# Output projection and last layer of an attention block from rounded fp32 pairs to norm-scaled fp16 pairs

## The chip, the cores and the metric

One NeuronCore of one Trainium2 chip runs the whole kernel. The metric is the device time of one execution in microseconds; of several executions the median is taken. The kernel before needs 1552.88 us (three executions, 1550.75 to 1553.57).

The engines are named as in the profile: PE is TensorE's matmuls and PEld its weight loads, DVE is VectorE, ACT is ScalarE, POOL is GpSimd, SP is SyncE, which issues most DMAs. SBUF is the on-chip memory and PSUM the memory into which PE writes.

## What is computed

One block of multi-head latent attention (2048 positions, width 512, 16 heads), followed by a residual and layer norm, a linear layer, and a residual and layer norm again. All inputs and outputs are fp32.

```python
cq  = rms_norm(x @ w_qa.T, q_a_ln_w);   q = (cq @ w_qb.T)            # 16 heads x (128 + 64 rotary)
ckv = x @ w_kva.T;                      ckv_l = rms_norm(ckv[..., :128], kv_a_ln_w)
k_nope, v = split(ckv_l @ w_kvb.T)      # 16 heads x (128 + 128)
attn = softmax(causal(q_full @ k_full.T * 192 ** -0.5))
a = concat_heads(attn @ v) @ w_o.T
x = layernorm(x + a)
w = ffn_weight * scale_weight[:, None]
x = layernorm(x + x @ w.T + bias)
```

The kernel uses a rearranged form. The values of all heads are one latent matrix (128 wide), so each head's attention is taken over the latent rows, and value weight and output weight of a head are multiplied together once (`wvo`, 128 x 512 a head).

## The kernel before

**Pairs.** Every large product is made of two numbers for each operand: a high part `h`, which is the operand rounded to the product's type, and a low part `l`, the rest. Three products high x high, high x low and low x high are added in PSUM. Projections, scores and values use fp16 pairs, scaled so that both parts fit fp16's range: `split16` (L66) lets ACT write `h = scale * src` and DVE write `l = scale * src - h`. The output stage and the last layer use pairs of F32R, a rounded fp32 type: `split` (L71) does the same with a plain subtraction (L75), or with a scale (L77, L78).

**Order of the work.** The 2048 rows are handled in four blocks of 512 (`b`), the 16 heads in eight pairs (`p`). `units` (L896) runs attention for one block: for each pair and each of four tiles of 128 rows (`qt`), scores (L618), maximum (L655), exp (L670), the split of the normalized probabilities (L691 on ACT, L694 on DVE), a DMA that transposes them on SP's queue (L698), and, three such steps later, the products with the latent values (L747). The result of each pair goes to DRAM (`ot_d`). From block 1 on PE and SP execute in the written order; the order on ACT, DVE and POOL is made by the planner of the framework, except that from the second step of block 3 ACT and DVE are in written order too. DMAs handed to `put_off` wait in a list and are issued on SP's queue by `put_in`, after the next transpose.

**The output stage** starts inside the last pair of block 3. `value_output` (L281) multiplies value and output weight of a pair and splits the result into `wvo`; `latent_load` (L999) brings a pair's attention result back, into one of two buffers `o`, and `latent_split` (L1003) splits it into `oh` and `ol`, two buffers of each, or, for pairs 4 to 7 of the last block, into eight tiles of their own (`ohl`). `accumulate` (L1042) adds a pair to one of four PSUM tiles `acc` of 128 rows x 512: six products of 128x512 (L1046), three for each head.

In each block all pairs are added to the four tiles, pair by pair. The last block does so for pairs 0 and 1 only (`CUT = 2`); for the rest it goes tile by tile, so that the tiles end one after the other.

**The last layer.** When a tile is full, `residual` (L1133) adds the input rows, `first_norm` normalizes them (`layer_norm`, L1124: statistics on DVE, the inverse root on POOL, scaling on DVE), and `ffn` (L1144) is appended to a list `late`. It has two steps that `advance` (L1165) runs at written places between accumulation products: first four transposes by PE (L1147) and the split `xt`, then twelve products (L1157), residual (L1159), layer norm and the DMA out (L1161). The weights `fw` are scaled, loaded and split by `load_fw` (L1118) in four pieces after pairs 4 to 7 of the first block.

## Time and profile before

| view | value |
|---|---|
| median of three executions | 1552.88 us |
| profiled execution | 1551.89 us |
| its span, first to last instruction | 1550.1 us |
| granted TensorE clock, mean | 0.987 |
| busy share: PE, PEld, DVE, ACT, POOL | 96%, 65%, 75%, 60%, 22% |
| PE accumulation L1046: `oh`, `ol`, `ohl` | 144.0 us x448, 88.1 us x224, 24.5 us x96 |
| PE last layer L1157 | 46.7 us x192 |
| PE weight products L286 | 16.1 us x32 |
| ACT exp L670 | 324.0 us x320 |
| SP's DMA queue, share of 16 DMA engines | 69.4% |

Busy times of PE overlap, because matmuls are pipelined and their ends are modelled: a matmul of 128x512 is listed with some 0.4 us and starts 0.2 us after the one before. For PE, times from start to start are what to read. Times of the other engines are those of one instruction. An idle time is put down to the work that ended last before the engine went on.

### The profile page before, as it was taken

The numbers are of one execution on the slowest core, as the hardware profiler recorded it, in microseconds if no ns is written. First come the engines' busy times: TensorE is split into PE (matmuls) and PEld (weight loads), VectorE is DVE, ScalarE is ACT, GpSimd is POOL, SyncE is SP. The second block draws the span as 40 slices with busy tenths as digits, with TensorE's granted clock in tenths as the row PEclk, the third lists the DMA queues.
The fourth block names the chain that finished last, engine by engine and source line by source line (L and its number), as shares of the span: only waits on it lengthen the run. The fifth ranks groups of instructions, "written<-read, shape, count | busy, mean of one in ns | idle before, by whom it ended". The sixth has DMA issues, their size and how long they took to land. (4 is left out here: it accounts for less than half of the span.)

```text
span 1550.1 us, 24523 instructions
## 1 busy us (share of the span) xinstructions
PE 1488.9 (96%) x9100; PEld 1000.6 (65%) x9100; DVE 1164.4 (75%) x2181; ACT 927.3 (60%) x1684; POOL 344.5 (22%) x398
## 2 busy tenths in 40 slices
PE   8889888999999999999999999999999999999997
PEld 6667664666665566666665665665566656788886
DVE  4887788888888888888896777777777775455564
ACT  6677775766675777767766666666666664321120
POOL 4223211441306304050052202201300000032132
PEclk9899999999999999999999999999999999999999
DMA  5556465878897988878986887786788798433230
GB/s 198 147 137 180 129 165 117 154 152 165 167 189 143 169 164 154 159 149 160 197 152 131 154 154 145 145 163 134 145 163 179 145 217 206 140 122 117 95 116 34
DMA packets 614872, 234.56 MB, mean 151 GB/s; under 512 B 569696, under 2 KB 593248, under 8 KB 614112
## 3 DMA queue, kind: packets, MB, share of 16 engines
q1 hardware_dynamic: 613440, 231.26, 69.4%
q8 instruction: 71, 1.16, 0.3%
q10 hardware_dynamic: 1008, 1.18, 0.3%
q0 software_dynamic: 304, 0.56, 0.1%
q14 instruction: 49, 0.40, 0.1%
HBM read 62.33 MB, written 28.05 MB: 58 GB/s over the span
## 5 line engine op out<-in xcount | busy, mean ns | idle before, releaser
L618 PE MATMUL s<-Kn,qn 128*128 128x512 f16 (+5 forms) x1920 | 465.2, 349 | 25.3 <-ACT pr L670 14.3
L670 ACT ACTIVATE pr<-s,bias,er 128x1024 f32<-128x1024 f32 (+3 forms) x320 | 324.0, 1015 | 210.6 <-DVE bias L664 161.8
L694 DVE SCALAR_TENSOR_TENSOR hl<-pr,inv,hl 128x1024 f16<-128x1024 f32 (+7 forms) x320 | 354.0, 1119 | 40.1 <-ACT hl L691 35.9
L747 PEld LDWEIGHTS <-V 128*128 128x128 f16 x3264 | 319.0, 98 | 80.8 <-issue 6.6
L747 PE MATMUL o<-ring,V 128*128 128x256 f16 x3024 | 361.0, 273 | 0.3 <-DVE qn L69 0.3
L691 ACT ACTIVATE hl<-pr,inv 128x1024 f16<-128x1024 f32 (+7 forms) x320 | 294.3, 960 | 80.6 <-ACT pr L670 34.3
L618 PE MATMUL s<-Kp,pe 128*128 128x512 f16 (+5 forms) x1280 | 342.1, 349 | 0.0
L655 DVE TENSOR_REDUCE neg<-s 128x1 f32<-128x1024 f32 (+3 forms) x320 | 317.2, 991 | 17.6 <-PE s L618 14.4
L618 PEld LDWEIGHTS <-qn 128*128 128x128 f16 x1920 | 188.3, 98 | 173.5 <-issue 34.9
L618 PEld LDWEIGHTS <-pe 128*128 128x128 f16 x1280 | 125.4, 98 | 106.4 <-issue 0.5
L576 PE MATMUL ps_qn<-cq,wq 128*128 128x512 f16 (+1 forms) x594 | 141.2, 386 | 5.9 <-DVE inv L680 2.2
L1046 PE MATMUL acc<-wvo,oh 128*128 128x512 f32 x448 | 144.0, 402 | 2.0 <-ACT pr L670 2.0
L565 POOL TENSOR_TENSOR pe<-prod,ph 32x512 f16<-32x512 f32 x88 | 121.7, 1383 | 5.7
L558 POOL TENSOR_TENSOR prod<-prod 128x512 f32<-128x512 f32 x11 | 14.0, 1269 | 465.6 <-DVE prod L502 465.6
L576 PEld LDWEIGHTS <-wq 128*128 128x128 f16 x594 | 60.2, 102 | 70.0 <-issue 13.3
L682 DVE TENSOR_SCALAR inv<-sums 128x1 f32<-128x1 f32 x128 | 27.0, 211 | 101.0 <-ACT pr L670 100.6
L1046 PEld LDWEIGHTS acc<-wvo,oh 128*128 128x128 f32 x448 | 83.1, 188 | 23.5 <-issue 3.8
L1046 PE MATMUL acc<-wvo,ol 128*128 128x512 f32 x224 | 88.1, 393 | 0.0
L564 POOL CAST pe<-prod 32x512 f16<-32x512 f32 x88 | 68.7, 781 | 13.8 <-PE o L747 10.4
L497 PE MATMUL ps_pe<-cq,wpe 128*128 128x512 f16 (+1 forms) x306 | 69.5, 372 | 1.2 <-DVE wpe L69 0.9
L74 ACT ACTIVATE oh<-o 128x1024 fp32r<-128x1024 f32 x28 | 29.7, 1060 | 65.9 <-PE acc L1046 48.6
L752 ACT ACTIVATE ot<-o 128x256 f32<-128x256 f32 x128 | 48.2, 377 | 34.8 <-PE o L747 25.9
(180 smaller groups left out, 1589.6 us busy)
## 6 DMA issues: line engine op xcount, KB each, us to landing
ot_d<-ot SPq DMA_DIRECT2D x128, 128.0 KB, 2.4
o<-ot_d SPq DMA_DIRECT2D x32, 512.0 KB, 3.6
wq<-wq_d SPq DMA_DIRECT2D x30, 384.0 KB, 3.8
wpe<-wpe_d SPq DMA_DIRECT2D x15, 384.0 KB, 3.8
wo<-in_wo_dram SPq DMA_DIRECT2D x4, 1024.0 KB, 5.5
x<-in_x_dram SPq DMA_DIRECT2D x16, 256.0 KB, 3.9
out_dram<-xb SPq DMA_DIRECT2D x16, 256.0 KB, 2.0
xr<-in_xT_dram SPq DMA_DIRECT2D x12, 256.0 KB, 3.5
```

What stands on the lines that cost most here:

```text
L497: nc.tensor.matmul(ps, w[:, i, lt, x * P : (x + 1) * P], cq[:, k, lt, cols], start=n == 0, stop=n == 3 * LT - 1)
L564: nc.gpsimd.tensor_copy(pe[32 * x : 32 * x + 32, j, :], rp[q, x, :])
L565: nc.gpsimd.tensor_tensor(pe[64 + 32 * x : 96 + 32 * x, j, :], rp[q, x, :], ph[q, 0, x, :], ALU.subtract)
L576: nc.tensor.matmul(ps, w[:, i, lt, j * P : (j + 1) * P], cq[:, k, lt, cols], start=n == 0, stop=n == 3 * LT - 1)
L618: nc.tensor.matmul(ps[:, :w], lhs, K[:, i, c0 : c0 + w], start=n == 0, stop=n == 4)
L655: nc.vector.tensor_reduce(neg[:, ti : ti + 1], v, axis=AX.XY, op=ALU.max, negate=True)
L670: nc.scalar.activation(pr[:, c0 : c0 + n * w].rearrange("p (a c) -> p a c", a=n), v, AF.Exp, bias=bias, scale=r, accum_out=sums[:, ti : ti ...
L691: nc.scalar.activation(hl[:, 0, c], pr[:, c], AF.Copy, scale=inv)
L694: nc.vector.scalar_tensor_tensor(hl[:, 1, c], pr[:, c], inv, hl[:, 0, c], ALU.mult, ALU.subtract)
L747: nc.tensor.matmul(ps[:, :256], vt[:, i, k % 4, :], v[:, :, l, k, :], start=n == 0, stop=n == 3 * kts - 1)
L752: nc.scalar.activation(ot, ps[:, :256], AF.Copy)
L1046: nc.tensor.matmul(acc, l[:, t, c], state["wvo"][p][:, i, j, :], start=p == 0 and j == 0 and n == 0, stop=p == NPAIR - 1 and j == 1 and n ...
```

## The change

Names and line numbers are those of the kernel before.

*Scales.* The new pairs are fp16, so each operand gets a scale from a norm. The attention result is scaled by `kvo` = key/value norm weight / its norm x 2^-12, `wvo` by `wscale` = 32768 / (norm of all value weights x norm of all output weights), the last layer's weights by `fscale` = 32768 / their norm, and its input by 1024. The products of these scales are taken back in `residual` (`back`) and after the last layer's products (`fback`).

```diff
+    kvo, wscale, back, fscale, fback = ...   # const tiles [P, 1] F32, in place of kvln_o
         root(kvn, tot)
+        rk = small.tile([P, 1], F32, tag="rf", name="rk")
+        nc.vector.reciprocal(rk, kvn)
+        nc.vector.tensor_scalar(kvo, kvln, rk, O_DOWN, ALU.mult, ALU.mult)
```

*Norms of the output weights.* A new generator reads both weights once more, in ten pieces of 128x1024 (512 KB). One step runs after the second head of each step `qt` of block 1, from pair 2 on. Its pool `nw` has two buffers and lives in block 1.

```diff
+    def output_norms(pool):
+        pieces = [a["wv"][:, 8 * i : 8 * i + 8] for i in range(2)] + [a["wo"][:, 2 * i : 2 * i + 2] for i in range(8)]
+        sums = small.tile([P, 10], F32, tag="osum", name="osum", bufs=1)
+        held = []
+        for n in range(len(pieces) + 1):
+            if n < len(pieces):
+                w = pool.tile([P, 1024], F32, tag="nw", name=f"nw{n}")
+                put_off(w.rearrange("p (a c) -> p a c", a=8 if n < 2 else 2), pieces[n])
+                held.append(w)
+            if n:
+                w = held.pop(0)
+                nc.scalar.activation(w, w, AF.Square, accum_out=sums[:, n - 1 : n])
+            yield
+        yield
+        ps = psum["m"].tile([P, 512], F32, tag="m", name="ps_on")
+        nc.tensor.matmul(ps[:, :10], ones, sums, start=True, stop=True)
...
+            root(f[:, i : i + 1], tot[:, i : i + 1])
...
+        nc.vector.reciprocal(r, f)
+        nc.vector.tensor_scalar(wscale, r[:, 0:1], r[:, 1:2], W_O, ALU.mult, ALU.mult)
+        nc.vector.tensor_scalar(back, f[:, 0:1], f[:, 1:2], kvn, ALU.mult, ALU.mult)
...
+                        if b == 1 and p >= 2 and j == 1:
+                            next(norms, None)
```

*Splits.* All F32R tiles of this stage become F16 (`wvo`, `oh`, `ol`, `ohl`, `fw`, `xt`). In the last block pairs 2 to 7 have tiles of their own, not 4 to 7.

```diff
-            split(ps, wvo[:, 0, j, :], wvo[:, 1, j, :], kvln_o)
+            split16(ps, wvo[:, 0, j, :], wvo[:, 1, j, :], wscale)
-        if b == NB - 1 and p >= 4:
+        if b == NB - 1 and p >= 2:
-        split(state.pop(("o", b, p)), oh, ol)
+        split16(state.pop(("o", b, p)), oh, ol, kvo)
```

*Last layer's weights.* `load_fw` becomes a generator of four steps, run after pairs 4 to 7 of the first block: the four loads into a tile of their own; four multiplications and four Squares; the norm; the four splits.

```diff
+        for kt in range(KT):
+            nc.vector.tensor_tensor(fraw[:, kt], fraw[:, kt], fsc, ALU.mult)
+            sq = pc.tile([P, HID], F32, tag="xb", name=f"fsq{kt}", bufs=2)
+            nc.scalar.activation(sq, fraw[:, kt], AF.Square, accum_out=sums[:, kt : kt + 1])
+        yield
+        ps = ps_f.tile([P, HID], F32, tag="ff", name="ps_fn")
+        nc.tensor.matmul(ps[:, :KT], ones, sums, start=True, stop=True)
...
+            split16(fraw[:, kt], fw[:, 0, kt, :], fw[:, 1, kt, :], fscale)
```

*Residual, norm and last layer in `n` parts.* `parts(n)` cuts the 512 columns into `n` slices. `layer_norm` takes statistics and writes its result part by part. The last layer's products go through all high x high and high x low terms first and through low x high after them.

```diff
-        nc.vector.tensor_tensor(x, acc, x, ALU.add)
+        for i, c in enumerate(parts(n)):
+            nc.vector.scalar_tensor_tensor(x[:, c], acc if n == 1 else acc[i], back, x[:, c], ALU.mult, ALU.add)
...
+        for c in range(0, KT, KT // cuts):
+            k4 = slice(c, c + KT // cuts)
+            for kt in range(c, c + KT // cuts):
+                nc.tensor.transpose(pt[:, kt, :], x1[:, kt * P : (kt + 1) * P], ident)
+            split16(pt[:, k4], xt[:, 0, k4], xt[:, 1, k4], X_UP)
...
+        terms = [(l, i, kt) for ls in (((0, 0), (0, 1)), ((1, 0),)) for kt in range(KT) for l, i in ls]
+        for c in parts(cuts):
+            for n, (l, i, kt) in enumerate(terms):
+                nc.tensor.matmul(
+                    ps[:, c], xt[:, l, kt, :], fw[:, i, kt, c], start=n == 0, stop=n == len(terms) - 1
+                )
+            nc.vector.scalar_tensor_tensor(xb[:, c], ps[:, c], fback, xb[:, c], ALU.mult, ALU.add)
+        layer_norm(xb, xb, cuts)
+        for n, c in enumerate(parts(cuts)):
+            (nc.scalar if n else nc.sync).dma_start(out[0, t * P : (t + 1) * P, c], xb[:, c])
```

*The last 128 rows.* In the last block pairs 0 and 1 are added to three tiles. The fourth is filled at the end, in two halves of columns, each in a PSUM tile of its own and with all eight pairs; the two steps of the row tile before run between them.

```diff
-                for t in range(4):
+                for t in range(3 if last else 4):
                     accumulate(accs[t], p, t, *cuts[b, p])
...
-            for t in range(4):
+            for t in range(3):
                 for i, p in enumerate(range(CUT, NPAIR)):
                     accumulate(accs[t], p, t, *cuts[b, p])
...
+            ends = [accs[3], ps_a.tile([P, HID], F32, tag="acc", name="acc3_4")]
+            for i, c in enumerate(parts(2)):
+                for p in range(NPAIR):
+                    accumulate(ends[i], p, 3, *cuts[b, p], c)
+                    if (i, p) in ((0, 6), (1, 2)):
+                        advance()
+            halves = [ends[i][:, c] for i, c in enumerate(parts(2))]
+            late.append(ffn(4 * b + 3, first_norm(b, 3, residual(b, 3, halves, 2), 2), 2))
```

## The prediction

> **What bounds the kernel now.** I read the page's slices first, then the stretches of the output stage, then the chain of waits in order of time, then the timeline of TensorE (PE).
>
> ```profile
> span 1550.1 us, 24523 instructions
> ...
> PE   8889888999999999999999999999999999999997
> ...
> DVE  4887788888888888888896777777777775455564
> ACT  6677775766675777767766666666666664321120
> ```
>
> PE is the bound nearly everywhere. After slice 33 (about 1290 us) ACT and DVE fall to half or less and PE stays at 9: the output stage. Its stretches, columns PE, PEld, DVE, ACT, POOL busy, granted clock, DMA share, GB/s:
>
> ```profile
> 1367.07:1424.04 56.97, 56.97 (x258) 46.65 (x257) 30.44 (x44) 10.89 (x12) 12.45 (x20) 1.00 0.35 111
> 1424.04:1480.80 56.76, 56.76 (x256) 46.48 (x255) 30.23 (x44) 10.89 (x12) 12.44 (x20) 1.00 0.34 111
> 1480.80:1535.74 54.94, 54.42 (x252) 44.43 (x251) 28.77 (x50) 9.27 (x12) 14.46 (x23) 1.00 0.22 75
> 1535.74:1550.10 14.36, 6.62 (x28) 4.40 (x26) 6.84 (x13) 0.60 (x1) 3.61 (x7) 0.95 0.10 37
> ```
>
> The first runs from one block's first transposes to the next block's, so it holds one block: 192 accumulation products (L1046), 48 of the last layer (L1157), 16 transposes (L1147). PE has no idle time in it and the clock is full. In all 54.94 us of the third there is one short wait, and only the last 14.4 us are a chain over several engines. So the price of this stage is the pitch of its products, start to start. The chain and the timeline give both pitches:
>
> ```profile
> 1343.65 23.41 PE acc L1046 x102
> 1367.07 0.44 PE tp L1147 x4
> ```
>
> ```profile
> 1281.52 0.81 PE L618 MATMUL s<-Kn,qn 128*128 128x512 f16 x3
> 1282.17 0.59 PE L618 MATMUL s<-Kp,pe 128*128 128x512 f16 x2
> 1282.60 0.81 PE L618 MATMUL s<-Kn,qn 128*128 128x512 f16 x3
> ```
>
> Rounded fp32: 23.41/102 = 0.2295; over the whole block (56.97 - 4 x 0.44)/240 = 0.2300 us. The fp16 score products, also 128x512 and also with a new weight load for each, start five in 1282.60 - 1281.52 = 1.08: 0.216 us.
>
> **The change, part by part.** The sum is made against the profiled execution: 1551.9 us, of which 1550.1 are the span, 1.0 under the median of 1552.9.
>
> *Pitch.* Between 1293.43 (from where the chain stays with PE and its feeders) and the end of the accumulation at 1535.5 lie 762 of the 768 accumulation products (six are earlier) and 180 of 192 of the last layer (12 come in the tail). 942 x (0.2300 - 0.2160) = **-13.2**. The transposes (L1147) and weight products (L286) stay fp32 and cost what they did. ACT does one 128x1024 copy per split as before (L74, 1.06). DVE does a scalar_tensor_tensor in place of a subtraction: 1.27 (L694, 128x1024) against 1.23 in the last blocks; the scaled residual 0.75 (L78) against 0.69. DVE is busy 30 of 57 us there, so these 0.1 us cost nothing; without that cover, 28 late splits and 16 residuals would be about 2 us.
>
> The Trainium skill speaks against this term: "TensorE: Matmul & The Clock Gate", section "Step-by-step: what each phase is for", has a stream of products cost "purely `N cycles`", and its specifications name the same 512 columns for all types; by that both kinds would take N/2.4 plus about 2.5 ns = 0.216 us and this term would be 0. The fp16 rows agree with it and the rounded fp32 rows do not, so I go by the rows.
>
> *Norm scales in block 1.* New: ten loads of 512 KB on SP's queue, ten ACT Squares of 128x1024, one small PE product, two reductions, six further DVE operations of one column, four on POOL. Exps of block 1 start every 3.63 us (24 from 317.6 to 404.8), so a pair of heads is 7.27 us, of which ACT is busy 56.21/85.00 = 66%: 4.8 us, 2.5 spare. A Square is about 1.1 plus 0.19 for its sum (L691 and L670): 1.25 with overlap. One per pair fits into the spare, if its load has landed. It is issued behind a transpose (1.5 us on SP) and the Square follows one head later; at 3.6 us to landing (o<-ot_d, also 512 KB) the Square waits 1.5 + 3.6 - 3.63 = 1.5, and what is queued behind it is the next head's exp, whose PSUM tile PE waits for. Ten times (1.5 + 1.25 - 2.5) = 2.5; with a Square placed after the landing, 0. I take **+1.5**. The loads also crowd the transposes: 5.24 MB at the 284 GB/s moved at share 0.89 (1300 to 1320) are 16.4 us of all queues, on 0.83 x 85 = 71: 87 of 85. The 2 us of backlog stay under the three pairs (22 us) by which values trail scores; without that lag they would cost 2. PE's small product comes two pairs after the last Square, and the scales are first used near 1255; POOL's and DVE's parts hide behind that.
>
> *Last layer's norm.* Four Squares (0.69 + 0.19) and one PE product between the sixth and seventh pair of block 0, where a pair takes 5.5 us and the chain of four multiplications (0.69 each) and the last Square takes 3.6. Fits, with **+0.3** for the product itself; up to 3 if DVE's queue has splits ahead. The fp16 splits follow at about 1357, first use is at 1370. The start gets two DVE operations more: **+0.2**.
>
> *Last block.* In the third stretch PE now reaches pair 2 earlier: twelve products (2.6 us) of the last 128 rows move behind all others, on top of the pitch. Its feeders are also freed: pairs 2 and 3 get their own split tiles and wait for no product. Counted from block 2's end, a load (3.5) and its split (1.06 + 1.23) take 6 us in each of two buffers; pair 5 is split at 17 while PE asks at 15, pair 7 at 23 against 21. In place of the one wait (0.5 by the waits, 0.7 in starts) I expect 1.5: **+0.8**, between -0.7 and +2.
>
> *Tail.* Before, the last twelve last-layer products of the row before ran at 1535.5 to 1538.3, under the DVE and POOL chain. Now both steps of it come before the end of the accumulation: 12 x 0.216 = +2.6 on PE's path. The last accumulation in halves costs 96 x 0.109 (L747, 256 columns) against 48 x 0.216: **+0.1**. After it the residual and statistics work on half of the columns (0.44 + 0.42 against 0.70 + 0.70): -0.5. The normalized halves, turns, splits, products and second residual could overlap by halves, but each of the two PSUM tiles is one bank. What the trace shows of such a bank is this:
>
> ```profile
> 12.57 0.28 DVE L331 COPY kvr<-ps_kv 128x128 f32<-128x128 f32 x1
> ...
> 12.88 0.22 ACT L334 ACTIVATE junk<-ps_kv 128x64 bf16<-128x64 f32 x1 [0.92 <-DVE kvr L331]
> ...
> 13.23 0.29 DVE L336 TENSOR_TENSOR rot<-ps_kv,csk 128x128 f32<-128x128 f32 x1 [0.38 <-ACT junk L334]
> ```
>
> Two engines that only read different columns of one tile take turns. If PE takes turns too, its second pair of turns waits for the first half's ACT and DVE (0.38 + 0.44), and its second half of products for DVE's 0.44. Worked through from the first norm's start, PE's products end at 5.8 us (before: 1538.37 to 1543.67, 5.3); then 0.44 + 0.42 in place of 0.70 + 0.70, and two half norms, 0.76, for one of 0.55: 8.7 against 8.5. With full overlap it would be about 7.0. So the tail is +2.6 - 0.5 + 0.2 = **+2.3**, between +0.6 (overlap) and +5 (if PE, idle for 2.6 us, restarts at the 0.50 clock of the first 12 to 14 us and its 24 products double). The row is two readers, not a writer, but it is the nearest, so I take turns.
>
> On the writer the Trainium skill has a rule, "PSUM — Partial Sum Buffer", section "PSUM bank collisions raise a hardware error": guard by bank and quadrant, not by address, for writers as for readers. By it the tail is +2.3, without it +0.6; no row before shows a PE write beside a read.
>
> Sum: -13.2 + 1.5 + 0.3 + 0.2 + 0.8 + 0.1 + 2.3 = -8.0: 1543.9 on the profiled execution, 1544.9 on the median. I forecast **1544.5**.
>
> **The rivals.**
> 1. *The halves do overlap* (0.15): tail +0.6, so 1542.8. For it: the two halves of the residual have separate banks. Against it: the rows above.
> 2. *The feeders become the bound* (0.12): loads, ACT and DVE fall behind in the blocks. For it: ACT waited 4.00 us for a load at 1302.92, and for products only because it was ahead; in the last block the margins are 1 to 2 us. Against it: ACT is at 19% in a full block. Four more microseconds: 1548.5.
> 3. *Squares block ACT* (0.08), the slower side: in block 1 a load lands after 6.6 us (the 512 KB load of cs there), not 3.6. Each Square then waits 4.5 us with exps behind it; ten times (4.5 + 1.25 - 2.5) = 32, less the three score tiles that PE runs ahead (10.9): +21 in place of 1.5, so 1564. For it: loads go behind transposes on one queue that is 0.83 full. Against it: ACT's order there is planned, not written out. It makes the kernel slower from a wait of 2.4 us per Square on: 10 x (2.4 + 1.25 - 2.5) = 11.5 against the 9.5 that the rest gains.
> 4. *The pitch isn't the type's* (0.05): accumulation stays at 0.230 for a reason of the stage, and the change brings only its costs: 1552.9 + 5.2 = 1558. Against it: L618 and L576 hold 0.216 with the same shape in the same kernel.
>
> **How the numbers follow.** My forecast has 0.60. A measurement of this kernel can't tell less than 0.2% (3.1 us) from no change. Faster: forecast 0.59, rival 1 0.15, half of rival 2 0.06: 0.80. Slower: rivals 3 and 4 but 0.02 that end within the bound, and 0.01 of the forecast: 0.12. The rest, 0.08, is no change. The range reaches from all bounds at their good end (-13.2 - 0.7 + 0.6 + 0.3 + 0.1 = -12.9, and 1 us of spread: 1539) to feeders and tail at their bad end (1551).
>
> **What would show it.** L1046 and L1157 at 0.216 start to start, blocks of some 53.6 us; ACT Squares in block 1 with waits for loads under 2 us and no PE wait behind them; one wait of 1 to 2 us in the last block; a tail of about 14 us from the last accumulation product, with PE and DVE in turns on the last tile. I am wrong if the pitch stays, if ACT waits longer for the loads, or if other blocks of attention change by more than 2 us.

## The result, and the profile after

| | before | changed |
|---|---|---|
| median, 17 executions each, in turns | 1552.88 us | 1556.01 us |
| lowest to highest | 1550.66 to 1554.55 | 1552.96 to 1559.17 |
| profiled execution, span | 1551.89, 1550.1 | 1558.61, 1556.8 |

The ratio is 1.0025, with a 95% interval of 1.0018 to 1.0032: slower by 3.1 us in the medians. Of all executions below one, 1710.69 us of `g2_const_halves` at a granted clock of 0.846, was in a slower state and is left out. Forecast were 1544.5 and a range of 1539 to 1551. The profiled execution of the changed kernel lies 2.6 us above its median, and that of the kernel before 1.0 below, so its parts sum to more than 3.1.

The page of the changed kernel, the slices of its span (40, tenths):

```profile
span 1556.8 us, 24722 instructions
...
PE   8889888998999999999999999999999998999997
...
DVE  5887787887888888888887777777777775465564
ACT  6677675666765776767775665665666665422220
```

PE falls to 8 in slice 10 (350 to 389 us), which was full before; the 8 in slice 34 is the start of the output stage, with waits that the kernel before has too. To see where the program falls behind, I paired each score product (L657 now, L618 before) with its like in the other trace; the written order of PE gives every one the same place in both:

| stretch, by the time before | started later by, in the stretch |
|---|---|
| up to 347 us | +0.35 |
| 347 to 435 us: block 1, where the Squares run | **+10.17** |
| 435 to 1261 us: the rest of attention | +0.57 |
| output stage (what is left of the span) | **-4.39** |

**Block 1.** The stretch of the Squares before and after (columns: PE, PEld, DVE, ACT, POOL busy, granted clock, DMA share, GB/s), and ACT's waits in it:

```profile
319.00:404.00 85.00, 85.00 (x556) 54.13 (x554) 72.66 (x155) 56.21 (x90) 38.28 (x36) 1.00 0.83 157
```

```profile
319.00:404.00 85.00, 76.10 (x487) 47.19 (x485) 65.91 (x137) 59.03 (x98) 33.66 (x33) 1.00 0.99 202
```

```profile
ACT nw L311 <- DMA nw<-in_wo_dram: 11.1, 8, 2.8
...
ACT nw L311 <- DMA nw<-in_wv_dram: 4.7, 2, 3.0
```

PE had no idle time and now has 8.9 us. All ten Squares wait for their loads, 15.8 us together. ACT's timeline shows what stands behind such a wait (the bracket is the idle time before, and what ended it):

```profile
370.77 1.08 ACT L709 ACTIVATE pr<-s,bias,er 128x896 f32<-128x896 f32 x1
...
374.71 1.06 ACT L311 ACTIVATE nw<-nw 128x1024 f32<-128x1024 f32 x1 [2.76 <-DMA nw<-in_wo_dram]
...
375.77 1.02 ACT L730 ACTIVATE hl<-pr,inv 128x896 f16<-128x896 f32 x1
376.70 1.18 ACT L709 ACTIVATE pr<-s,bias,er 128x1024 f32<-128x1024 f32 x1
```

The exp that starts at 376.70 had nothing left to wait for; it stood behind the Square. Behind that exp ACT has the copy `ot` of a finished value product, and this copy is what PE waits for next:

```profile
378.30 1.14 PE L786 MATMUL o<-ring,V 128*128 128x256 f16 x9 [1.57 <-ACT ot L791]
```

**Output stage.** One full block, from its first transposes to the next block's, and the last block around its wait; then the chain of waits:

```profile
1375.64:1429.19 53.55, 53.55 (x259) 25.33 (x257) 29.73 (x45) 11.58 (x12) 15.79 (x25) 1.00 0.38 123
...
1481.00:1485.00 4.00, 4.00 (x12) 1.48 (x11) 2.50 (x3) 1.49 (x2) 3.42 (x4) 0.58 0.68 203
```

```profile
1405.88 23.31 PE acc L1087 x108
1429.19 0.44 PE tp L1220 x4
```

A block takes 53.55 us where it took 56.97, and 23.31/108 = 0.2158 us is the pitch of a product: the gain is there. It is given back behind it. In the last block (ACT, DVE and PE):

```profile
1474.46 1.15 ACT L71 ACTIVATE ohl<-o,kvo 128x1024 f16<-128x1024 f32 x1 [4.99 <-DMA o<-ot_d]
...
1475.51 1.13 ACT L71 ACTIVATE oh<-o,kvo 128x1024 f16<-128x1024 f32 x1
...
1478.41 2.28 DVE L72 SCALAR_TENSOR_TENSOR ol<-o,kvo,oh 128x1024 f16<-128x1024 f32 x1
...
1480.75 0.39 PE L1087 MATMUL acc<-wvo,ol 128*128 128x512 f16 x1 [2.76 <-DVE ol L72]
```

ACT splits pair 2 (`ohl`) ahead of pair 1 (`oh`), which PE needs first; PE waits 2.76 us, and for the next four microseconds the granted clock is 0.58: some eight products start 0.427 us apart instead of 0.216, 1.7 us. The end:

```profile
1535.01 2.75 PE L1229 MATMUL ff<-fw,xt 128*128 128x512 f16 x12
...
1541.08 0.48 DVE L1206 SCALAR_TENSOR_TENSOR x<-acc,back,x 128x256 f32<-128x256 f32 x1
...
1543.81 0.66 PE L1220 MATMUL tp<-ident,x 128*128 128x128 f32 x2 [2.77 <-DVE x L1200]
...
1544.93 0.42 DVE L72 SCALAR_TENSOR_TENSOR xt<-tp,xt 128x256 f16<-128x256 f32 x1 [0.94 <-ACT xt L71]
1545.41 0.69 PE L1220 MATMUL tp<-ident,x 128*128 128x128 f32 x2 [0.93 <-DVE xt L72]
1545.89 2.77 PE L1229 MATMUL ff<-fw,xt 128*128 128x256 f16 x12
...
1549.30 1.74 PE L1229 MATMUL ff<-fw,xt 128*128 128x256 f16 x12 [0.64 <-DVE xb L1232]
...
1553.24 0.73 DVE L1200 TENSOR_SCALAR xb<-xb,mv,lnr 128x256 f32<-128x256 f32 x2 [0.98 <-POOL lnr L332]
```

The twelve products of the row before run at 1535.01, ahead of the end. The halves take turns: the second pair of transposes waits 0.93 us for DVE, which reads other columns of the same tile, and the second twelve products wait 0.64. From the last residual to the last norm it is 12.90 us, before 11.13.

### The profile page after: what moved, and what is told of

Its sections match the earlier page's. It is cut to its first block, busy times and chain, and to the rows that moved or that the text cites. A ratio compares the mean times of both kernels' runs of the same rounds, so it can differ in the third digit from the quotient of the medians.

```text
span 1556.8 us, 24722 instructions
## 1 busy us (share of the span) xinstructions
PE 1481.7 (95%) x9164; PEld 923.4 (59%) x9164; DVE 1169.7 (75%) x2199; ACT 941.9 (61%) x1713; POOL 352.2 (23%) x404
## 5 line engine op out<-in xcount | busy, mean ns | idle before, releaser
L657 PE MATMUL s<-Kn,qn 128*128 128x512 f16 (+5 forms) x1920 | 466.0, 349 | 26.2 <-ACT pr L709 15.7
L657 PE MATMUL s<-Kp,pe 128*128 128x512 f16 (+5 forms) x1280 | 342.6, 350 | 0.0
L657 PEld LDWEIGHTS <-qn 128*128 128x128 f16 x1920 | 188.3, 98 | 175.5 <-issue 36.3
L657 PEld LDWEIGHTS <-pe 128*128 128x128 f16 x1280 | 125.4, 98 | 106.8 <-issue 0.3
L1087 PE MATMUL acc<-wvo,oh 128*128 128x512 f16 (+1 forms) x424 | 125.7, 379 | 2.1 <-ACT pr L709 2.1
L1087 PE MATMUL acc<-wvo,ol 128*128 128x512 f16 (+1 forms) x212 | 80.2, 378 | 2.8 <-DVE ol L72 2.8
L1087 PEld LDWEIGHTS <-oh 128*128 128x128 f16 x424 | 41.7, 99 | 51.4 <-issue 8.3
L603 POOL CAST pe<-prod 32x512 f16<-32x512 f32 x88 | 68.8, 782 | 14.7 <-PE o L786 11.3
L71 ACT ACTIVATE xt<-tp 128x512 f16<-128x512 f32 (+1 forms) x17 | 9.7, 571 | 91.8 <-PE tp L1220 85.5
```

Source lines behind the costliest of these rows:

```text
L603: nc.gpsimd.tensor_copy(pe[32 * x : 32 * x + 32, j, :], rp[q, x, :])
L657: nc.tensor.matmul(ps[:, :w], lhs, K[:, i, c0 : c0 + w], start=n == 0, stop=n == 4)
L1087: nc.tensor.matmul(acc[:, cols], l[:, t, c], state["wvo"][p][:, i, j, cols], start=p == 0 and j == 0 and n == 0, stop=p == NPAIR - 1 and j ...
```

## The experiments

Each run is set beside executions of the kernel before on the same chip (medians 1552.2 to 1553.0). "Block 1", "rest" and "output" are the stretches of the table above; "chain" is the time from the start of the last residual to the end of the last norm. The stretch up to 347 us, in which these kernels differ by less than the spread, varied from -2.2 to +0.6.

| run | median us | ratio, 95% interval | block 1 | rest | output | chain |
|---|---|---|---|---|---|---|
| changed kernel | 1556.01 | 1.0025 [1.0018, 1.0032] | +10.2 | +0.6 | -4.4 | 12.9 |
| n1_const | 1546.91 | 0.9969 [0.996, 0.9979] | 0.0 | +0.6 | -4.2 | 13.2 |
| n3_loads | 1546.59 | 0.9964 [0.995, 0.9977] | +1.0 | -1.2 | -4.1 | 13.1 |
| n4_squares | 1545.43 | 0.996 [0.9947, 0.9973] | +0.1 | +0.2 | -4.0 | 13.0 |
| n2_lag | 1554.61 | 1.0015 [1.0005, 1.0025] | +9.2 | -2.0 | -4.0 | 13.2 |
| n5_lag_pin | 1550.23 | 0.9984 [0.9976, 0.9993] | +5.2 | -0.9 | -5.0 | 13.0 |
| t1_tail | 1549.93 | 0.998 [0.9971, 0.999] | +9.4 | -1.4 | -11.5 | 11.3 |
| t2_pin | 1554.76 | 1.001 [1.0001, 1.0019] | +10.4 | -0.1 | -8.1 | 12.2 |
| c0_plain | 1542.92 | 0.9939 [0.9926, 0.9952] | 0.0 | 0.0 | -7.2 | 13.0 |
| b0_on_later | 1555.26 | 1.0014 [1.0005, 1.0023] | +1.4 | +8.5 | -4.0 | 12.4 |
| b1_both | 1549.10 | 0.9971 [0.9958, 0.9983] | +1.2 | +6.5 | -11.4 | 11.3 |
| b2_const_tail | 1540.74 | 0.992 [0.9908, 0.9933] | 0.0 | +1.1 | -11.5 | 11.3 |
| b3_halves | 1550.60 | 0.9986 [0.9977, 0.9995] | +1.6 | +8.6 | -10.1 | 9.7 |
| f0_order | 1573.25 | 1.0137 [1.0124, 1.015] | +9.2 | +16.2 | -4.8 | 12.4 |
| f3_full | 1566.41 | 1.0093 [1.008, 1.0106] | +9.8 | +17.4 | -10.6 | 13.0 |
| f2_halves | 1565.57 | 1.0081 [1.0068, 1.0094] | +9.3 | +17.6 | -12.0 | 9.7 |
| g2_const_halves | 1540.29 | 0.9925 [0.9912, 0.9938] | 0.0 | +1.1 | -12.5 | 9.7 |
| h1_lag_full | 1544.78 | 0.995 [0.9936, 0.9963] | +5.6 | -0.8 | -11.8 | 11.3 |
| h2_lag_halves | 1543.50 | 0.9949 [0.9936, 0.9961] | +5.4 | -1.2 | -12.7 | 9.7 |

### Block 1: loads, Squares, or the wait between them

Theory: ACT, which works in order, is parked on loads that have not landed. Rivals: the ten loads crowd the DMA queues, or the Squares' own 12.5 us of ACT work is too much. `n1_const` has neither loads, Squares nor their norm (the scales come from two constants); `n3_loads` keeps the loads and leaves the Squares out; `n4_squares` squares a tile of ones ten times and loads nothing:

```diff
+        nc.vector.memset(wscale, W_O / (45.254834 * 22.627417))   # n1_const, in place of the whole generator
...
-                nc.scalar.activation(w, w, AF.Square, accum_out=sums[:, n - 1 : n])   # left out in n3_loads
...
-                put_off(w.rearrange("p (a c) -> p a c", a=8 if n < 2 else 2), pieces[n])   # left out in n4_squares
```

> Leaves out the norms of the two output weights: no loads, no Squares, no product for them in block 1; the two scales come from constants. If block 1's norm work costs what the trace of the changed kernel shows there (scores 10.5 us late by the end of block 1), the time falls by 9 to 11 us from 1556.0 to 1545 to 1547, and scores of block 2 start within 1 us of the kernel before. If that delay came from elsewhere in the change (a different plan of the order because of new tiles and scales), it stays near 1556.

> Leaves out the Squares; the ten loads are kept and read by nobody, the sums are constants. If the loads' crowding of the transposes on SP's queue is the cost, scores stay 5 to 10 us late and the time near 1556. If ACT's waits or work are the cost, the time falls to 1545 to 1548.

> Leaves out the ten loads; ten Squares of the same size run at the same places on a tile of ones, which no transfer fills. If ACT's work is the cost, the time stays near 1556. If only the wait for the landing is, the time falls to 1545 to 1548. In between, each Square costs what exceeds ACT's 2.5 us of spare per pair of heads.

Without both, block 1 loses nothing and the kernel is 1546.91 us, 9.1 less than the changed kernel. The loads alone are nearly free, +1.0. The windows row of that run:

```profile
319.00:404.00 85.00, 84.53 (x552) 53.76 (x550) 71.41 (x151) 55.33 (x89) 38.28 (x36) 1.00 1.09 216
```

The queues are as busy as in the changed kernel, or busier (1.09 against 0.99), and PE still has 84.53 of 85. So the loads by themselves are not the cost.

`n4_squares` doesn't answer its half of the question, though its time (1545.43) is in the range set for it. Its Squares on ACT (the durations are least, median and most in ns, then the starts of the first and the last):

```profile
L312 ACT ACTIVATE nsq<-one x10: 1045/1062/1092, 204.6 to 229.9; 128x1024 f32<-128x1024 f32 x10
```

With no load to wait for, the planner put them into block 0, some 130 us earlier than in the changed kernel. Block 1 of that run has neither loads nor Squares, so its +0.1 says nothing about Squares there. What is left is the wait or the Squares' work in block 1. If it is the wait, Squares that come later must be nearly free. Two runs put each one step later (three buffers `nw`); the second also holds it to its place in the program:

```diff
-            if n:
+            if n > 1:
-                nc.scalar.activation(w, w, AF.Square, accum_out=sums[:, n - 1 : n])
+                tc.keep_in_program_order(nc.scalar.activation(..., accum_out=sums[:, n - 2 : n - 1]))  # n5 only
```

> The Square of a piece is issued one step (7.3 us) later, with three buffers in place of two; the same loads and Squares. If ACT's wait for the landing, with exps behind it, is the cost (15.8 us of ACT waits in ten Squares), the waits fall under 2 us in all and the time falls by 8 us or more, to 1546 to 1548. If ACT's own work on the Squares (12.4 us) or the crowded DMA queues are the cost, waits fall but the time stays within 2 us of 1556.

> As n2_lag, and each Square is also held behind what is written before it on ACT. (In n2_lag the ten Squares stand at the same ten places of ACT's order as in the changed kernel: the planner puts them where it takes the load as landed.) Here nine of ten stand four to eight ACT instructions later, with all loads and Squares kept. If a Square's wait for its load, with exps behind it, is the cost, ACT's 15.8 us of waits fall below 4 us and the time falls by 7 to 10 us from 1556.0, to 1546 to 1549. If loads and Squares together are too much for block 1 without any wait, it stays above 1553.

`n2_lag` still waits 15.9 us and loses 9.2: in ACT's program the ten Squares stand within one place of where they stood. The reading that fits: the planner puts an instruction where its model takes the operands as ready, whatever the program's order, and in the model the loads (4.2 to 5.3 us to landing in the changed kernel's trace) land earlier. The Squares of `n4_squares`, ready at once and 130 us early, fit it too; the model itself no run shows. Held in place, no Square waits, and up to 408 us, with all ten Squares done, the loss is 1.3. The rest, 3.9, comes at 412 us, from a new place (PE's timeline; the stretch after it):

```profile
412.44 0.39 PE L315 MATMUL ps_on<-osum,ones 128*128 128x10 f32 x2 [1.86 <-DVE qn L72]
```

```profile
412.40:417.00 4.60, 4.56 (x23) 2.65 (x24) 2.73 (x10) 2.30 (x5) 2.27 (x4) 0.67 1.02 205
```

The ones product of the norms takes a PSUM tile of `m` whose last reader, DVE's split of `qn`, is 1.86 us late; then the clock is 0.67 for some microseconds.

### The ones product elsewhere

`b0_on_later` is `n5_lag_pin` with one more `yield` ahead of the ones product, so that it comes a step later. `f0_order` holds the Squares in program order without the lag and runs the product in block 3:

```diff
-        yield   # left out in f0_order; b0_on_later has one more
         ps = psum["m"].tile([P, 512], F32, tag="m", name="ps_on")
...
-                        if b == 1 and p >= 2 and j == 1:
+                        if b == 1 and 8 <= 4 * p + qt < 19 and j == 1 or (b, p, qt, j) == (3, 2, 0, 1):   # f0_order
```

> The changed kernel with the Squares one step later and held in program order (as in the run before with both), and the ones product of the norms (L315) one step later still, away from the step whose fill has just taken the PSUM tiles of 'm'. Theory: what block 1 still lost in that run was this product's wait of 1.86 us for a PSUM tile, and the slower clock behind it: the scores then reach 414 us at most 2 us later than before (there 5.2), and the time falls by 2.5 to 4 us, from 1550.2 to about 1546.5. Rival: the rest comes from the ten loads or from the Squares' 12.4 us of work, not from the product's place: scores at +4 to +5 and 1549 to 1551.

> The changed kernel with the Squares held in program order, not put one step later, and the ones product taken out of block 1 into block 3 (third pair). The order of ACT then differs from the kernel without norms in 10 rows, all in block 1, against 42 up to the last block in the run with the product one step later. Theory: the losses at 507 and 850 us came from that order, and are gone: the scores at 1261 us stand at most 2 us behind the kernel before's, and the time is that of the constants (1546.9) plus 0 to 2, 1547 to 1549. Rival: the Squares now stand where their loads (4.4 to 6.0 us to landing) have not landed, or the product in block 3 waits as it did in block 1: 1550 to 1553.

`b0_on_later` met its expectation in block 1 (+1.4), and that answers the question left above. Three runs have all ten loads and all ten Squares in block 1 and no Square that waits: `b0_on_later` loses 1.4 there, `b1_both` 1.2 and `b3_halves` 1.6 (the last two are described below), of which the loads alone were 1.0. Where the Squares wait, 15.8 us together in the changed kernel, 15.9 in `n2_lag`, 11.0 in `f0_order` and 12.7 in `f3_full`, block 1 loses 9.2 to 10.2. So it is the wait.

The time of `b0_on_later` missed by 9 us: the score products fall back 4.7 us by 507 us and 6 us at 834 to 846, in blocks that the edit doesn't touch. ACT and PE at the first place:

```profile
498.52 1.44 ACT L731 ACTIVATE hl<-pr,inv 128x576 f16<-128x576 f32 x2 [1.94 <-DMA ring<-hl]
```

```profile
505.09 1.23 PE L658 MATMUL s<-Kn,qn 128*128 128x512 f16 x3 [2.34 <-ACT pr L710]
```

Before, the next head's exp stood ahead of these splits. Now they come first and ACT is parked until a transpose has left their buffer; DVE's low half waits 2.31 us behind it, the next maxima behind that, and their exps are late. Against `n5_lag_pin`, ACT's order differs between 414 and 545 us and nowhere else, for one `yield` some 90 us before the loss; PE's order is the same there. That cannot be the cause of the second loss, 300 us later. There the first exp of block 3 waits, in `b0_on_later` and then in `n5_lag_pin`:

```profile
843.81 1.20 ACT L710 ACTIVATE pr<-s,bias,er 128x1024 f32<-128x1024 f32 x1 [6.47 <-DMA ring<-hl]
```

```profile
836.34 1.20 ACT L709 ACTIVATE pr<-s,bias,er 128x1024 f32<-128x1024 f32 x1 [1.16 <-DMA ring<-hl]
```

The first waits for the last transpose of block 2, the second for the one before it. `b1_both` has the long wait too (6.39 us). Why the exp waits for another transfer in these runs stays open.

`f0_order` shows both halves at full size. Block 1 loses 9.2 again, with 11.0 us of Squares waiting: held in order but without the lag, they come too early. Its rival, a wait in block 3, came far dearer than the 3 to 6 us set for both: the rest of attention loses 16.2. PE at the ones product, then DVE, then POOL, then PE again:

```profile
968.76 0.60 PE L314 MATMUL ps_on<-osum,ones 128*128 128x10 f32 x2 [5.25 <-DVE prod L540]
```

```profile
969.48 0.15 DVE L317 TENSOR_REDUCE otot<-ps_on 128x1 f32<-128x8 f32 x1
987.51 0.17 DVE L322 RECIPROCAL or<-of 128x2 f32<-128x2 f32 x1 [17.88 <-POOL of L166]
```

```profile
976.65 9.64 POOL L603 TENSOR_TENSOR pe<-prod,ph 32x512 f16<-32x512 f32 x8
986.37 1.10 POOL L166 TENSOR_TENSOR of<-rt_t,half 128x1 f32<-128x1 f32 x2
```

```profile
993.04 1.12 PE L656 MATMUL s<-Kn,qn 128*128 128x384 f16 x3 [11.04 <-ACT pr L708]
```

The ones product itself waits 5.25 us for its PSUM tile. Then DVE is parked for 17.88 us on a root of one column that POOL has queued behind eight operations on `pe` (9.64 us); the maxima, and so the exps, and so PE's score tiles stand behind it, and PE waits 11.04 us. The two waits make the 16.2. But the losses at 507 and 844 us are gone (the score products stay at +8.8 from 435 to 941), though loads and Squares are in block 1 as before, and ACT's order departs from that of `n1_const` in block 1 only. So the norms by themselves don't bring those losses. For the one at 507 us the order that the theory named fits; what brings the one at 844 us, these runs don't show.

### The last 128 rows

`t1_tail` gives the last 128 rows the order of the kernel before (full width, pairs 0 and 1 not put off, the step of the row before behind the end); own tiles for pairs 2 to 7 stay. `t2_pin` is the changed kernel with ACT's split of pair 2 held behind that of pair 1. `c0_plain` has the constants, the old end, and own tiles for pairs 4 to 7 only; `b2_const_tail` the same with 2 to 7.

```diff
-                for t in range(3 if last else 4):
+                for t in range(4):
...
-            ends = [accs[3], ps_a.tile([P, HID], F32, tag="acc", name="acc3_4")]
...
-            late.append(ffn(4 * b + 3, first_norm(b, 3, residual(b, 3, halves, 2), 2), 2))
```

```diff
+        pin = tc.keep_in_program_order if (b, p) == (NB - 1, 2) else lambda ins: ins   # t2_pin
+        pin(nc.scalar.activation(oh, o, AF.Copy, scale=kvo))
...
-        if b == NB - 1 and p >= 2:
+        if b == NB - 1 and p >= 4:   # c0_plain
```

> Undoes the order of the last 128 rows alone: pairs 0 and 1 are added to all four tiles, the last tile is filled in full width, its residual, norm and last layer are whole, and the twelve products of the row tile before come behind the last accumulation. Norm work in block 1 stays. If the order is what costs in the tail (2.6 us of products on PE's path, 1.3 us of longer chain) and, by the shorter lead of pairs 0 and 1, causes the 2.8 us wait of the last block, the time falls by 6 to 8 us to 1548 to 1550. If only the tail itself is, 3 to 4 us; if the halves do save time, it rises by 1 to 2.

> In the last block the high split of pair 2 is held behind the high split of pair 1 on ACT, as written; nothing else differs. If the wait of the last block (2.8 us, and 1.7 us at the lower clock after it) comes from pair 2's split standing before pair 1's on ACT, with its load not landed, the wait falls below 1 us, the clock stays at 1.00 and the time falls by 3 to 4.5 us to 1552. If it comes from the shorter lead alone, nothing changes.

> Pitch alone: fp16 pairs with constant scales (no norms of the output weights), the last 128 rows as in the kernel before and own tiles for pairs 4 to 7 only. The prediction's term for the pitch, 942 products by 0.014 us, gives 1552.5 - 13.2 + 0.5 = 1540, with a last-block wait of at most 1 us. If the stage's feeders took part of it back, 1543 to 1547.

> Constants in place of the norm sums (no loads, no Squares, no ones product) and the old order of the last 128 rows: the pitch of fp16 alone, and the last block's tiles. 1552.2 - 13.2 is 1539.0, with the other small terms (last layer's norm 0.3, start 0.2) 1539.5; range 1538.5 to 1541. If it is 1543 as in the run in which pairs 2 and 3 shared the buffers, the own tiles are worth nothing. The norm's true price is this run against the one with both: theory under 2 us.

The old end is worth 6.1 us in medians (1556.01 to 1549.93), the same 6.2 with the constants (1546.91 to 1540.74), and 7.1 to 7.3 in the output stage of the profiled executions: the new end, not the pitch, costs it. In `t2_pin` the 2.76 us wait falls to 0.7 and the output stage gains 3.7, but the median falls by 1.3 us only (1556.01 to 1554.76), where 3 to 4.5 were expected: the profiled execution lies 1.9 us below its median there and 2.6 above it in the changed kernel, so their difference says too much. In `c0_plain` PE waits more for its feeders than with own tiles for pairs 2 and 3 (3.4 us in three waits before two pairs) and the clock falls in the tail: 1542.92 against 1540.74. The intervals overlap, [0.9926, 0.9952] and [0.9908, 0.9933], and a part is the clock's, so the 2 us are no measured worth of the own tiles. That edit alone, on the changed kernel, wasn't tried: pairs 0 and 1 hold the shared buffers until the end there.

Is the halving bad, or only its bank and its place? `b3_halves` gives each half a PSUM tile of its own for transposes and products, puts only the second half off, and leaves the twelve products of the row before behind the end:

```diff
-        pt = ps_f.tile([P, KT, P], F32, tag="tp", name=f"tp{t}")
         for c in range(0, KT, KT // cuts):
+            pt = ps_f.tile([P, KT, P], F32, tag="tp", name=f"tp{t}_{c}")
...
-                for p in range(NPAIR):
+                for p in range(0 if i else CUT, NPAIR):
                     accumulate(ends[i], p, 3, *cuts[b, p], c)
-                    if (i, p) in ((0, 6), (1, 2)):
+                    if (i, p) == (0, 6):
                         advance()
```

> The same with, besides, the last 128 rows in the order of the kernel before (full width, not put off, the step of the row before behind the end); the own tiles of pairs 2 to 7 stay. Theory: the two losses are separate and add up: 1546.5 less what the output stage regained in the run with the old tail (11.5 - 5 = 6.5) is 1540, with 1539 to 1543. Rival: the regained time of the old tail was in part the attention part's spread between executions (its attention delta was 4 us smaller than the changed kernel's): then 1543 to 1545.

> As the one with both, but the last 128 rows in halves of columns again, with a PSUM tile of its own for each half in the transposes and in the last layer's products, only the second half put off (pairs 0 and 1 take the first half in their place), and the 12 products of the row before behind the end as in the kernel before. Theory: the halving lost because its two halves shared one bank and took turns, and because it put all of pairs 0 and 1 off and 12 products ahead of the end: without these it is 1 to 2 us faster than the run with both, 1539 or less. Rival: there is nothing to be had, since the last chain (norm, transposes, splits, 24 products, norm, store) is only partly divided and each half costs its own fixed times: same as the run with both within 0.7, or slower.

`b1_both` came to 1549.1, not 1540: the attention part lost 6.5 as in `b0_on_later`, the output stage gave the 11.4 expected. In `b3_halves` the chain is 9.7 us against 11.3, the theory's 1.6, but the whole was no faster: a wait of 2.18 us in the last block, with eight products at half clock behind it, took it back. So the comparison was made again with that wait mended (`f2_halves` against `f3_full`, and with constants `g2_const_halves`):

> The same with the old order of the last 128 rows (full width) and, in the last block, ACT's high split of the third pair held behind that of the second. Theory: 1540.7 (constants with the old tail) plus 0 to 2 for the norms less 0 to 1.5 for the wait at the second pair: 1539.5 to 1542. Rival as above: 1543 to 1546.

> The same, but the last 128 rows in halves of columns with a PSUM tile for each half, only the second half put off, and the 12 products of the row before behind the end. Theory: the halving gains what the last chain showed, 1.6 us, when nothing else differs: 1 to 2 us below the run at full width, 1538 to 1541. Rival: the later pairs' splits then wait elsewhere and take it back: same within 0.7.

> Constants in place of the norms, the rest as in the run with halves: the floor, 1538 to 1539.5. The norms' price with the order kept is the run with halves less this one: theory 0 to 2 us, where the changed kernel paid 9.1 (1556.0 less 1546.9).

The first two missed their times by the 25 us of `f0_order`, which they share. Their output stages, -12.0 and -10.6, and those with constants, -12.5 and -11.5, say about 1 us for the halves. In medians it can't be told: 1540.29 [0.9912, 0.9938] against 1540.74 [0.9908, 0.9933].

### Both mended

`h1_lag_full` is `n5_lag_pin` with the old end, `h2_lag_halves` the same with halves in tiles of their own and the pin of `t2_pin`.

> The run with the Squares one step later and held in order (1550.2, ones product left at its place in block 1), with the old order of the last 128 rows besides. ACT's order up to the last block is that run's, row for row. Theory: the attention part costs 2 us as there, the output stage gives 11.5 as in the run with the old end: span 1550.1 + 2.15 - 11.5 = 1540.7, time 1542 to 1544. Rival: parts don't add, because the rest of the program is planned anew: 1545 or more.

> The same with halves of columns at the end, a PSUM tile for each half, only the second half put off, the 12 products of the row before behind the end, and the split of the third pair held behind the second's in the last block. Theory: 0.5 to 1.5 us below the run at full width (the last chain is 1.6 shorter, and a wait of the last layer's first row stands in the last block). Rival: same within 0.5, as the two runs with constants were (1540.7 and 1540.5).

1544.78 and 1543.50: the first is 0.8 above what was expected of the sum, the second 1.3 below the first, though their intervals don't tell them apart. Both beat the kernel before by 0.5% (ratios 0.9936 to 0.9963 and 0.9936 to 0.9961) and the changed kernel by 11 to 12.5 us. The end of `h2_lag_halves`:

```profile
1528.95 2.75 PE L1232 MATMUL ff<-fw,xt 128*128 128x512 f16 x12
1529.15 0.48 DVE L1209 SCALAR_TENSOR_TENSOR x<-acc,back,x 128x256 f32<-128x256 f32 x1 [3.72 <-PE acc L1090]
...
1531.88 0.73 PE L1223 MATMUL tp<-ident,x 128*128 128x128 f32 x4 [0.18 <-DVE x L1203]
...
1532.77 3.09 PE L1232 MATMUL ff<-fw,xt 128*128 128x256 f16 x24 [0.15 <-ACT xt L71]
...
1538.13 0.74 DVE L1203 TENSOR_SCALAR xb<-xb,mv,lnr 128x256 f32<-128x256 f32 x2 [0.98 <-POOL lnr L332]
```

The twelve products of the row before cover the norm chain, and four transposes and 24 products run without turns. Some 3 us remain to the 1540.3 without norms; the ones product's wait and the clock behind it (3.9 us at 412 us in `n5_lag_pin`) are the likeliest place, and no run here removed these without shifting the planned order.

## Why the prediction was wrong

**The step that failed is "Norm scales in block 1": +1.5 forecast, +10.2 in the profile, 9.1 in medians** (changed kernel less `n1_const`). The wait itself was right: 1.5 us per Square predicted, 15.8/10 = 1.6 measured. The price was wrong twice. I let 2.5 us of ACT's spare time per pair of heads swallow wait and Square, and then took less than the 2.5 that even this gave. But a share of idle time is not a reserve at one point: ACT idles because exps wait for their maxima (11 such waits, 13.6 us, before in this stretch), and a parked ACT shifts that whole loop. The spare does swallow the work: the runs whose Squares don't wait lose 1.2 to 1.6 with loads and all, which is what I had forecast for the term. It doesn't swallow a wait at the head of an in-order queue. Of 10 x (1.6 + 1.25) = 28 us some 18 were swallowed. The 0 for "a Square placed after the landing" assumed that the planner would put it there.

**Rival 3 is what happened, in a milder form.** Its mechanism (exps behind a parked Square) holds; its landing of 6.6 us was too long (4.2 to 5.3), and its point from which it decides, 2.4 us per Square, too high: at 1.6 the term alone took all but 3 us of the pitch's gain. My argument against it, that ACT's order is planned, was the reason for it.

**Pitch, -13.2: right.** A block is 3.42 us shorter, 240 x 0.014 = 3.36 forecast. In `b2_const_tail`, with the old end and without norms, the output stage gives 11.5, a wait of 1.6 us in the last block included (0.5 before); `c0_plain`, which shares buffers, gives 7.2. The sum had 180 of the last layer's products in this term; 12 of them run in the tail and were priced there, so it is 168, a difference of 0.2 us. Rival 4 is out.

**Last layer's norm +0.3, start +0.2: too small to see.** The norm's product takes 0.12 us in the chain; the start varies more than that.

**Last block, +0.8: mis-sized.** The wait is 2.9 us by the starts (2.76 by the waits) in place of 0.7, and 1.7 us of half clock stand behind it: +3.9. I had DMA, split and demand in the sum, but not that the planner could put pair 2's split ahead of pair 1's, nor the clock. Rival 2's 4 us more came about from another cause.

**Tail, +2.3: mis-sized.** The 2.6 for the twelve products and the turns on one bank were right. The chain grew by 1.8, not by 0.2 less 0.5: PE, idle for 2.77 us, restarted at half clock, twelve products of 256 columns taking 2.77 us; that was in the upper bound. The split store gave 0.4 back: +4.0. The Trainium skill's rule ("PSUM — Partial Sum Buffer", section "PSUM bank collisions raise a hardware error"), to guard by bank and quadrant, or simply by bank, and not by address, fits: PE waits for a reader of other columns of the tile (0.93 us above), and with a tile for each half the wait is gone. Rival 1 was not given a chance by the kernel; `h2_lag_halves` gave it one, and the chain is 9.7.

The terms now sum to -13.2 + 10.2 + 0.3 + 0.2 + 3.9 + 0.1 + 4.0 = +5.5; the profiled span grew by 6.7. Of the difference 0.4 stands in attention away from the Squares (+0.9 measured, against the 0.5 of the two small terms) and 0.8 in the output stage (-4.4 against -5.2); from what, no run shows.

## What to carry to other kernels

Before adding work to an in-order engine, price the wait that it brings, not its busy time: ask what lands when, whether the order there is written or planned, and what stands behind it. Where a planner orders an engine, place a consumer of a DMA late and hold it there, and look at the orders and waits far behind the edit too. When an experiment takes away what an instruction waits for, look where the planner then puts that instruction before reading the result. Halving a last tile can pay only if each half has its own PSUM tile and PE keeps other work to cover the chain; here that came to about 1 us in the output stage of the profiled executions, and was not told in medians.

## What the runs showed of the hardware

The clock fell to half after PE waits of 2.76 us in the last block and of 1.86 us at 412 us. The length of a wait doesn't decide it. In `f3_full` and `b1_both` the tails are alike: both have the same last twelve products of row 14, then starts 1.825 us and 0.96 us apart, then the last twelve. In one these run at half clock and in the other at full; the chain is 13.0 and 11.3 us.

What differs is where the waits fall. In all 20 traces the granted clock changes only on a grid of 3.413 us, whose phase differs from execution to execution. The windows rows on that grid, first the two stretches of `f3_full`, then two of `b1_both`:

```profile
1551.20:1554.61 3.41, 1.28 (x8) 0.53 (x6) 2.21 (x5) 0.60 (x1) 2.04 (x4) 1.00 0.00 0
1554.61:1558.02 3.41, 3.41 (x9) 1.17 (x8) 1.02 (x2) 0.00 (x0) 0.52 (x1) 0.50 0.21 77
```

```profile
1530.10:1533.51 3.41, 2.15 (x10) 0.78 (x8) 2.39 (x6) 0.00 (x0) 0.77 (x2) 1.00 0.00 0
1533.51:1536.92 3.41, 2.53 (x13) 1.32 (x14) 2.06 (x5) 0.60 (x1) 2.01 (x3) 1.00 0.00 0
```

In `f3_full` both waits fall into one stretch, PE is busy for 1.28 us of it, and the next runs at 0.50. In `b1_both` they are split over two, busy for 2.15 and 2.53 us, and the clock stays at 1.00. Over all traces, of the stretches at full clock followed by full clock none had PE idle for more than 2.03 us; those followed by half clock had it idle for 1.74 us or more, but for the first 10 us of the program. So what goes with the fall is the idle time within one stretch (between 1.74 and 2.03 us both cases occur), and since the phase differs from execution to execution, whether waits share a stretch is chance. The Trainium skill ("TensorE: Matmul & The Clock Gate", section "🔬 Part 1: The HAM clock gate (the "warmup" mystery)") has a free-running window of 3413 ns decide on the clock; the rows agree. Its warning of gaps over about 3.4 us (section "HAM oscillation — how this bites in real kernels") is too lenient here: 1.86 us was enough.

The DMA share of a stretch can stand at 1.09 with PE losing 0.5 us of 85 and block 1 as a whole 1.0 us (`n3_loads`): here a full queue by itself cost little, an engine parked on it ten times as much.
